# VectorE's convolution sums in PSUM, and a round plan for the work between scans

## The chip, the core and the metric

The kernel runs on one core of a Trainium2 chip. The core has TensorE (PE, matrix products, with its weight loads shown apart as PEld), VectorE (DVE), ScalarE (ACT), GpSimd (POOL) and the SyncE queue (SP), which here issues all DMAs. SBUF and PSUM are the on-chip memories; PE writes its results to PSUM. The metric is the device time of one execution in microseconds (us), the median of several runs; lower is better.

## What is computed

Four layers work on four images of 64x64 positions with 96 channels. The first two are state-space layers, the last two attention without softmax and a small feed-forward net with rounded values. The change concerns the first two (and, through a shared class, the start of the last two). One such layer, cut to what matters:

```python
xz = einsum('bhwc,ec->bhwe', group_norm(x), in_proj_w)      # 96 -> 2 x 192
xp, z = split(xz, 2)
xc = conv_general_dilated(xp, conv_w, 3x3, 'SAME', feature_group_count=192)
xc = silu(xc + conv_b)                                       # u in the kernel
xs = four orders of xc: by rows, by columns, and both reversed
delta, B, C = softplus(...), ..., ...                        # small products of xs
h_l = exp(delta_l * A) * h_(l-1) + delta_l * u_l * B_l       # 16 states per channel
y = sum over states of h * C, over the four orders, + D * u
y = layernorm(y) * w + b
y = y * silu(z)
x = x + einsum('bhwd,cd->bhwc', y, out_proj_w)
```

The convolution is depthwise: each channel is a sum of nine shifted copies of its image, each times a weight of that channel (nine "taps").

## The kernel before

**Units.** A layer takes the four images in two pairs, so there are four units (layer 0 pair 0, layer 0 pair 1, layer 1 pair 0, layer 1 pair 1). `PairScan` runs the recurrence of a unit over all positions, states and orders, in steps of 1024 positions. Before each scan stands a stage, `between_scans` (line 128). Before the first scan it only makes the inputs of unit 0. Before the other three it is "joint": `Inputs` makes the next unit's inputs while `Outputs` finishes the unit whose scan just ended. The outputs of the last unit are made in `token_layers`, by `one_by_one` (line 484), beside the start of the attention layers.

**Order.** `InOrder` (line 48) keeps each compute engine's instructions in the order in which the program issues them, so an instruction that waits holds up all behind it on its engine. SP's DMAs are not wrapped so; the framework places them.

**Inputs.** A pair's 192 channels of two images are held in three images `imgs[0..2]` of 128 partitions each (the third has the last 64 channels of both). The input comes in 16 pieces (`BEATS`) of 512 positions. `project` (line 302) multiplies a piece with the weights three times (PSUM tiles `ips`, tag `mm`), and ACT copies it out four times: twice into the images, twice through SiLU into `zs`, which goes to DRAM as `zg`. `fold` puts the group norm into the weights and `in_shift`, clears the images' borders and makes nine diagonal matrices `diag`.

**Convolution.** `jobs` (line 325) yields one tap at a time. `CONVS` names which rows of which image go to which engine, as (image, first row, rows):

- `vector`: nine DVE instructions over SBUF; the first multiplies and adds the bias, the others do `to = view * weight + to` (`SCALAR_TENSOR_TENSOR u<-img,par,u`). Sixteen rows make 128x1024 elements.
- `tensor`: nine products with `diag`, summed in a PSUM tile `cps`.
- `gpsimd`: ACT multiplies a tap into `parts`, POOL adds it to `u`.

After the taps ACT applies SiLU. `Handout` hands out taps by `SHARES`, a sixth of a beat's share at each of the six `fill()` calls of a beat.

**Outputs.** In groups `g` of 256 positions: load `zt`, `xr`, `ys`; `measure` (DVE statistics of `ys`), `scale` (through `rstd_of`, line 65: DVE adds epsilon into `ln_ve`, POOL takes the power -0.5 into `ln_rs`), `shift` (DVE), `normalise` (ACT, in place in `ys`), `turn` (PE transposes into `pt`), `scaled_back` (ACT, into `gt`), `gate` (POOL multiplies `gt` by `zt`), `project` (PE, into `po`), `store` (DVE adds `xr`, and takes the next norm's statistics `gn_stats`; in layer 1 ACT copies `po` instead). A beat of the loop in `between_scans` holds steps of the groups `beat - 1`, `beat` and `beat + 1`, with `fill()` between them. `close` ends the norm of the next layer's input.

**Start of the scan.** `scan.begin` makes the scan's first chunk of projections and its first `delta` and `du`; the loop takes a step of it at each `fill()` from beat `BEGIN` on. `other` collects, in the first stage only, the statistics of the second pair.

[...]A joint stage gives five to the tag `mm`, two to `pt`, one to `po`.

Of the kernel before, what the change touches and what calls it, by code (L numbers as in the profile page):

```python
# [9 lines left out]
F32 = mybir.dt.float32  # L10
# [54 lines left out]
def rstd_of(nc, pool, var, shape, tag, half):  # L65

    ve = pool.tile(shape, F32, name=f"{tag}_ve", bufs=4)
    nc.vector.tensor_scalar(ve, var, EPS, None, ALU.add)
    rs = pool.tile(shape, F32, name=f"{tag}_rs", bufs=4)
    nc.gpsimd.tensor_tensor(rs, ve, half, ALU.pow)  # L70
    return rs
# [55 lines left out]

def between_scans(tc, cst, ident, half, pn, u, before, scan, after):

    with ExitStack() as stage:  # L130
        nc = InOrder(tc)
        outs, other, joint = None, iter(()), before is not None
        pieces = PIECES[joint]
# [10 lines left out]
        ins.fold()  # L144
        convs = [Handout(ins.jobs(engine), share) for engine, share in SHARES[joint].items()]
        beginnings = scan.begin(nc, ins.pp)
        for beat in range(-LEAD, BEATS + 1):
            now = outs is not None and 0 <= beat < BEATS
            past = outs is not None and beat > 0
            ready = pieces[beat + LEAD]  # L150

            def fill():
                if beat >= BEGIN[joint]:
                    next(beginnings, None)
                if beat < BEATS:
                    for one in convs:
                        one.go(ready)

            if past:
                outs.gate(beat - 1)  # L160
            fill()
            if now:
                outs.normalise(beat)
            if outs is not None:
                for g in range(0 if beat == -LEAD else beat + 2, min(beat + 3, BEATS)):
                    outs.load(g)
                if 0 <= beat + 1 < BEATS:
                    outs.measure(beat + 1)
                    outs.scale(beat + 1)
            fill()  # L170
            for piece in range(*pieces[beat + LEAD : beat + LEAD + 2]):
                if piece + 4 < BEATS:
                    ins.load(piece + 4)
                ins.project(piece)
            fill()
            if now:
                outs.turn(beat)
                outs.scaled_back(beat)
            fill()
            if past:  # L180
                outs.project(beat - 1)
            ready = pieces[beat + LEAD + 1]
            fill()
            if past:
                outs.store(beat - 1)
            if outs is not None and 0 <= beat + 1 < BEATS:
                outs.shift(beat + 1)
            fill()
            if beat >= 3:
                next(other, None)  # L190
        for _ in beginnings:
            pass
        while any([one.go(BEATS) for one in convs]):
            pass
        if outs is not None:
            outs.close()
        for _ in other:
            pass
# [3 lines left out]
    False: (0, 3, 5, 7, 9, 11, 13, 15, 16, 16, 16, 16, 16, 16, 16, 16, 16, 16, 16, 16),  # L202
    True: (0, 3, 5, 6, 8, 9, 11, 12, 14, 15, 16, 16, 16, 16, 16, 16, 16, 16, 16, 16),
}
LEAD = 1
BEGIN = {False: 4, True: 8}

CONVS = {
    False: {'vector': ((0, 0, 16), (2, 0, 16), (0, 16, 16), (2, 16, 16), (0, 32, 16), (2, 32, 16), (2, 48, 16), (0, 48, 16), (1, 56, 8)), 'tensor': ((1, 0, 8), (1, 8, 8), (1, 16, 8), (1, 24, 8), (1, 32, 8), (1, 40, 8), (1, 48, 8))},
    True: {'vector': ((0, 0, 16), (2, 0, 16), (0, 16, 16), (2, 16, 16), (0, 32, 16), (2, 32, 16), (2, 48, 16), (0, 48, 8)), 'tensor': ((1, 0, 8), (1, 16, 8), (1, 32, 8), (1, 48, 8), (1, 40, 8)), 'gpsimd': ((1, 8, 8), (1, 24, 8), (1, 56, 8), (0, 56, 8))},  # L210
}
SHARES = {False: {'vector': 9, 'tensor': 6}, True: {'vector': 5, 'tensor': 3, 'gpsimd': 3}}

class Handout:
# [5 lines left out]
    def go(self, beat):  # L220
        self.owed = min(self.owed + self.share / 6, self.share)
        while self.owed >= 1 and self.ready is not None and beat >= self.ready:
            self.owed -= 1
            self.ready = next(self.pieces, None)
        return self.ready is not None

class Inputs:

    def __init__(self, nc, tc, stage, cst, ident, half, pn, u, spare, joint, layer, pr):
# [7 lines left out]
        self.pp = stage.enter_context(tc.tile_pool(name="a_ps", bufs=5, space=PSUM))  # L237
# [4 lines left out]
        self.xs, self.xns = {}, {}  # L242
# [59 lines left out]
    def project(self, beat):  # L302

        nc, (c, i) = self.nc, divmod(beat, 2)
        mine, other = slice(D1 * i, D1 * i + D1), slice(D1 - D1 * i, 128 - D1 * i)
        cols, rows = slice(512 * c, 512 * c + 512), slice(1 + 8 * c, 9 + 8 * c)
        xn, zg = self.xs.pop(beat), self.layer.zg[self.pr]
        pss = []
        for q in range(3):
            ps = self.pp.tile([128, 8, HW], F32, name=f"ips{q}", tag="mm")  # L310
            nc.tensor.matmul(ps, self.wi[:, i, 128 * q : 128 * q + 128], xn, start=True, stop=True)
            pss.append(ps)
        shift = self.shift[:, i]
# [10 lines left out]

    def jobs(self, engine):

        nc, par = self.nc, self.layer.par
        for j, row, n in CONVS[self.joint][engine]:
            s, cols = j // 2, slice(HW * row, HW * (row + n))
            last = min(HW // 8 - 1, (row + n) // 8)  # L330
            after = 2 * last + (j > 0) + 1
            to = self.u[j][:, cols].rearrange("p (h w) -> p h w", w=HW)
            bias = par[:, s, P_CB : P_CB + 1]
            yield after
            if engine == "tensor":
                to = self.pp.tile([128, 8, HW], F32, name="cps", tag="mm")
            for tap in range(9):
                dy, dx = divmod(tap, 3)
                v = self.imgs[j][:, row + dy : row + dy + n, dx : dx + HW]
                weight = par[:, s, P_CONV + tap : P_CONV + tap + 1]  # L340
                if engine == "tensor":
                    nc.tensor.matmul(to, self.diag[:, tap], v, start=(tap == 0), stop=(tap == 8))
                elif engine == "vector" and tap == 0:
                    nc.vector.tensor_scalar(to, v, weight, bias, ALU.mult, ALU.add)
                elif engine == "vector":
                    nc.vector.scalar_tensor_tensor(to, v, weight, to, ALU.mult, ALU.add)
                elif tap == 0:
                    nc.scalar.activation(to, v, AF.Identity, scale=weight, bias=bias)
                else:
                    part = self.parts[:, tap % 2]  # L350
                    nc.scalar.mul(part, v, weight)
                    nc.gpsimd.tensor_tensor(to, to, part, ALU.add)
                yield after
            if engine == "tensor":
                nc.scalar.activation(self.u[j][:, cols], to.rearrange("p h w -> p (h w)"), AF.Silu, bias=bias)
# [562 lines left out]
class Rounds:  # L918

    def __init__(self):  # L920
        self.tasks = {}
# [397 lines left out]
```

## Time and profile before

| | |
|---|---|
| median of 3 runs | 10450.39 us (10448.65 to 10457.71) |
| the profiled execution | 10456.78 us, of which its instructions span 10454.9 us |
| granted TensorE clock, mean | 0.887 of full speed |
| busy share of the span | PE 76%, PEld 56%, DVE 92%, ACT 84%, POOL 89% |
| scan, POOL `h<-h,cb` | 3072 instructions, 7194.7 us |
| scan, DVE `h<-da,last,bp` | 2064 instructions, 4736.2 us |
| first stage | to 160.65 us |
| joint stages | 2455.7 to 2657.0, 4955.7 to 5159.1, 7452.6 to 7640.8 us |
| chain that ended last, by engine | ACT 34%, issue 20%, DVE 17%, PE 16%, POOL 11% |

The stage boundaries are from the timeline: from the end of DVE's last scan instruction to the start of its first `bp` product for the next unit. Busy time counts an instruction from start to end, with any wait that it spends after it has started. A group of instructions is named by what it writes and reads (`u<-img,par,u`), with the shape of what it writes. Since the in-order wrapper issues every instruction, nearly all groups carry its line, L61, and are told apart by their tiles.

### The profile page before, as it was taken

The numbers are of one execution on the slowest core, as the hardware profiler recorded it, in microseconds if no ns is written. First come the engines' busy times: TensorE is split into PE (matmuls) and PEld (weight loads), VectorE is DVE, ScalarE is ACT, GpSimd is POOL, SyncE is SP. The second block draws the span as 40 slices with busy tenths as digits, with TensorE's granted clock in tenths as the row PEclk, the third lists the DMA queues.
The fourth block names the chain that finished last, engine by engine and source line by source line (L and its number), as shares of the span: only waits on it lengthen the run. The fifth ranks groups of instructions, "written<-read, shape, count | busy, mean of one in ns | idle before, by whom it ended". The sixth has DMA issues, their size and how long they took to land.

```text
span 10454.9 us, 142148 instructions
## 1 busy us (share of the span) xinstructions
PE 7920.4 (76%) x47500; PEld 5900.9 (56%) x47500; DVE 9648.0 (92%) x6803; ACT 8817.8 (84%) x18798; POOL 9255.7 (89%) x5402
## 2 busy tenths in 40 slices
PE   7777777777777777777777777777777777777767
PEld 4655555554555555555455555555556555555555
DVE  8999999999999999999899999999899999999957
ACT  6888888887888888888788888888888888888868
POOL 3999999997899999999699999999789999999946
PEclk9898998988888998888888989898988898988978
DMA  4677777776577777777477777777757777777730
GB/s 138 205 213 215 218 221 219 221 220 185 185 211 210 219 221 213 219 219 215 160 207 212 218 214 218 223 218 220 203 178 209 215 217 218 218 218 220 219 104 25
DMA packets 903380, 2117.24 MB, mean 203 GB/s; under 512 B 330326, under 2 KB 639896, under 8 KB 704920
## 3 DMA queue, kind: packets, MB, share of 16 engines
q1 hardware_dynamic: 902648, 2108.15, 68.8%
q8 instruction: 377, 6.18, 0.3%
q14 instruction: 355, 2.91, 0.1%
HBM read 1946.42 MB, written 161.48 MB: 202 GB/s over the span
## 4 chain that ended last, share of the span: by engine, by line
ACT 34%; issue 20%; DVE 17%; PE 16%; POOL 11%; DMA 2%; SPq 1%; DVEq 0%; POOLq 0%; ACTq 0%
ACT x L61 14%; ACT da L61 12%; DVE h L61 9%; POOL h L61 8%; PE yp L61 6%; PE bp L61 5%; DVE bp L61 4%; ACT bp L61 2%; DVE u L61 1%; PE xps L61 1%; POOL dbu L61 1%; DMA cb<-crow 1%; PE dps L61 1%; ACT L61 1%; PE dups L61 1%
## 5 line engine op out<-in xcount | busy, mean ns | idle before, releaser
L61 POOL TENSOR_TENSOR h<-h,cb 128x1024 f32<-128x1024 f32 x3072 | 7194.7, 2366 | 230.5 <-issue 64.0
L61 DVE TENSOR_TENSOR_SCAN h<-da,last,bp 128x1024 f32<-128x1024 f32 x2064 | 4736.2, 2335 | 143.8 <-PE bp L61 19.7
L61 ACT ACTIVATE x<-dut,bt 128x128 f32<-128x128 f32 x12288 | 3495.0, 370 | 1.5 <-PE bp L61 1.3
L61 PE MATMUL yp<-ident,h 128*128 128x128 f32 x24576 | 3351.3, 296 | 10.5 <-POOL h L61 10.5
L61 PEld LDWEIGHTS yp<-ident,h 128*128 128x128 f32 x24576 | 3177.9, 156 | 125.7 <-issue 74.3
L61 ACT ACTIVATE da<-delta,amat 128x1024 f32<-128x1024 f32 x2752 | 3060.4, 1138 | 103.0 <-DVE h L61 97.8
L61 PE MATMUL bp<-ident,x 128*128 128x128 f32 x10240 | 1670.4, 315 | 1293.0 <-DVE h L61 950.2
L61 PEld LDWEIGHTS bp<-ident,x 128*128 128x128 f32 x10240 | 1352.8, 162 | 1857.3 <-ACT x L61 1004.3
L61 DVE TENSOR_TENSOR bp<-du,bp 128x1024 f32<-128x1024 f32 x1472 | 1780.1, 1213 | 260.8 <-PE bp L61 259.2
L61 DVE TENSOR_TENSOR_SCAN h<-da,bp 128x1024 f32<-128x1024 f32 x688 | 1537.5, 2274 | 45.6 <-ACT da L61 4.6
L61 PE MATMUL bp<-bparts,sel 96*128 96x512 bf16 x2944 | 924.7, 400 | 761.4 <-DVE h L61 742.7
L61 PEld LDWEIGHTS <-sel 96*128 96x128 bf16 x2944 | 226.3, 100 | 1557.9 <-DVE h L61 1048.7
L61 ACT ACTIVATE bp<-delta,amat 128x1024 f32<-128x1024 f32 x320 | 358.1, 1119 | 528.0 <-DVE h L61 526.2
L61 POOL TENSOR_TENSOR dbu<-du,bb 128x1024 f32<-128x1024 f32 x320 | 754.9, 2359 | 0.0
L61 DVE TENSOR_TENSOR_SCAN h<-bp,last,dbu 128x1024 f32<-128x1024 f32 x240 | 558.9, 2329 | 13.4 <-POOL dbu L61 12.7
L61 PE MATMUL xps<-u,wx 128*76 128x512 f32 x768 | 556.8, 811 | 0.0
L61 ACT ACT_TABLE_LOAD x392 | 502.9, 1283 | 11.3 <-DMA x<-xo 4.4
L61 POOL COPY last<-h 128x2 f32<-128x2 f32 x1152 | 215.4, 187 | 326.7 <-DVE h L61 309.8
L61 POOL TENSOR_TENSOR du<-delta,u 128x1024 f32<-128x1024 f32 x188 | 496.6, 2642 | 0.0
L61 PE MATMUL dps<-cdt,wdt 12*128 12x512 f32 x768 | 442.4, 656 | 0.0
L61 ACT COPY ysum<-yp 128x1024 f32<-128x1024 f32 x192 | 194.4, 1012 | 284.7 <-PE yp L61 284.7
L61 ACT COPY dut<-dups 128x512 f32<-128x512 f32 x384 | 220.6, 574 | 239.7 <-PE dups L61 239.7
(141 smaller groups left out, 6296.9 us busy)
## 6 DMA issues: line engine op xcount, KB each, us to landing
cb<-crow SPq DMA_DIRECT2D x1024, 1024.0 KB
cb<-crow SPq DMA_DIRECT2D x1024, 512.0 KB
bb<-crow SPq DMA_DIRECT2D x384, 256.0 KB
bb<-crow SPq DMA_DIRECT2D x128, 512.0 KB
y<-ysum SPq DMA_DIRECT2D x192, 256.0 KB
kept<-y SPq DMA_DIRECT2D x160, 256.0 KB
y<-ysum SPq DMA_DIRECT2D x64, 512.0 KB
zt<-zg SPq DMA_DIRECT2D x64, 384.0 KB
```

Of the source, the lines that this page charges most:

```text
L61: return self.tc.keep_in_program_order(getattr(self.engine, op)(*args, **kwargs))
```

## The change

Three things change together.

**The vector chunks.** They are all eight rows high (128x512 elements). ACT makes the first tap with the bias, into a PSUM tile `vps`[...]; DVE adds the other eight taps there; ACT's SiLU reads PSUM and writes `u`. The next chunk's first tap is issued after the fifth tap of the present one, and a chunk's SiLU after the fourth tap of the next. In a joint stage one chunk, (0, 56, 8), moves from `gpsimd` to `vector`.

**The order.** The six-part beats are replaced by a list of rounds (`Rounds`, moved up in the file). `plan` gives each step of an output group a round of its own, two rounds from group to group, with the load six rounds ahead of `measure`. A piece's products (`multiply`) and ACT's copies of it (`spread`) stand a round apart, and its taps may begin a round later. Every round ends with the handout of taps and, from round `BEGIN` on, one step of the scan's beginning. GpSimd's addition is handed out one step after ACT's product. The tail's `one_by_one` uses the same `plan`, which loads groups two rounds earlier than before.

**Small moves.** `ln_ve` goes to the engine that gates, POOL in joint stages and DVE in the tail. `po` shares the two buffers of `pt`; `mm` has four buffers in a joint stage and six in the first.

```diff
-def rstd_of(nc, pool, var, shape, tag, half):
+def rstd_of(nc, pool, var, shape, tag, half, engine):
-    nc.vector.tensor_scalar(ve, var, EPS, None, ALU.add)
+    engine.tensor_scalar(ve, var, EPS, None, ALU.add)
...
         ins.fold()
+        rounds, ready = Rounds(), {}
+        if outs is not None:
+            outs.plan(rounds, OUTS_FROM)
+        for piece in range(BEATS):
+            r = PIECES[joint][piece]
+            if piece + 4 < BEATS:
+                rounds.at(r, ins.load, piece + 4)
+            rounds.at(r, ins.multiply, piece)
+            rounds.at(r + 1, ins.spread, piece)
+            ready[r + 2] = piece + 1
         convs = [Handout(ins.jobs(engine), share) for engine, share in SHARES[joint].items()]
-        beginnings = scan.begin(nc, ins.pp)
-        for beat in range(-LEAD, BEATS + 1):
...
+        beginnings, pieces = scan.begin(nc, ins.pp), 0
+        for r, _ in enumerate(rounds.run()):
+            pieces = ready.get(r, pieces)
+            for one in convs:
+                one.go(pieces)
+            if r >= BEGIN[joint]:
+                next(beginnings, None)
+            if r >= 3:
                 next(other, None)
+        while any([one.go(BEATS) for one in convs]):
+            next(beginnings, None)
...
 PIECES = {
+    False: (0, 1, 3, 4, 6, 7, 9, 10, 12, 13, 15, 16, 18, 19, 21, 22),
+    True: (0, 2, 4, 6, 8, 10, 12, 14, 16, 18, 20, 22, 24, 26, 28, 30),
 }
+OUTS_FROM = 6
+PER_GROUP = 2
+BEGIN = {False: 10, True: 18}
...
-SHARES = {False: {'vector': 9, 'tensor': 6}, True: {'vector': 5, 'tensor': 3, 'gpsimd': 3}}
+SHARES = {False: {'vector': 6, 'tensor': 2.5}, True: {'vector': 4, 'tensor': 1.4, 'gpsimd': 1}}
...
-        self.pp = stage.enter_context(tc.tile_pool(name="a_ps", bufs=5, space=PSUM))
+        self.pp = stage.enter_context(tc.tile_pool(name="a_ps", bufs=4 if joint else 6, space=PSUM))
...
                 else:
                     part = self.parts[:, tap % 2]
                     nc.scalar.mul(part, v, weight)
-                    nc.gpsimd.tensor_tensor(to, to, part, ALU.add)
+                    yield after
+                    nc.gpsimd.tensor_tensor(rows, rows, part, ALU.add)
+                    continue
                 yield after
...
+    def vector_jobs(self, chunks):
+
+        nc, sums = self.nc, {}
+
+        def begin(i):
+            _, _, views, weights, bias = chunks[i]
+            sums[i] = self.pp.tile([128, 8, HW], F32, name="vps", bufs=2)
+            nc.scalar.activation(sums[i], views[0], AF.Identity, scale=weights[0], bias=bias)
+
+        def end(i):
+            nc.scalar.activation(chunks[i][1], sums.pop(i).rearrange("p h w -> p (h w)"), AF.Silu)
+
+        yield chunks[0][0]
+        begin(0)
+        for i, (after, _, views, weights, _) in enumerate(chunks):
+            for tap in range(1, 9):
+                yield after
+                nc.vector.scalar_tensor_tensor(sums[i], views[tap], weights[tap], sums[i], ALU.mult, ALU.add)
+                if tap == 4 and i > 0:
+                    end(i - 1)
+                if tap == 5 and i + 1 < len(chunks):
+                    yield chunks[i + 1][0]
+                    begin(i + 1)
+        yield BEATS
+        end(len(chunks) - 1)
...
+    def plan(self, rounds, start):
+        for g in range(BEATS):
+            rounds.at(max(start + PER_GROUP * g - 6, 0), self.load, g)
+            for r, task in enumerate((
+                self.measure, self.scale, self.shift, self.normalise, self.turn, self.scaled_back, self.gate,
+                self.project, self.store,
+            )):
+                rounds.at(start + PER_GROUP * g + r, task, g)
...
     def one_by_one(self):
         rounds = Rounds()
...
+        self.plan(rounds, 4)
         yield from rounds.run()
```

In `CONVS` a joint stage has 16 vector chunks of eight rows (before: seven of sixteen and one of eight), five tensor chunks (unchanged) and three for GpSimd (before: four). The first stage has 17 vector chunks of eight rows (before: eight of sixteen and one of eight) and seven tensor chunks (unchanged).

## The prediction

> **What bounds the kernel.** I read the busy digits of the page first, then busy time by stretch around the dips, then the groups of those stretches, and last their timeline.
>
> ```profile
> DVE  8999999999999999999899999999899999999957
> POOL 3999999997899999999699999999789999999946
> ```
>
> POOL has a dip at the start and three more, a quarter of the span apart. These are the stretches between scans, the only places that the change touches before the tail; the scans keep their instructions. From the timeline (last scan instruction on DVE to the first `bp` product of the next unit) they last to 160.65 us at the start, then 2455.7 to 2657.0 (201 us), 4955.7 to 5159.1 (203) and 7452.6 to 7640.8 (188): 753 us, 7% of the span, are in play. Columns: busy us and count per engine, granted clock, DMA share, GB/s.
>
> ```profile
> core 0: us, PE busy (x) PEld busy (x) DVE busy (x) ACT busy (x) POOL busy (x), PEclk, DMA share, GB/s
> 27.00:160.00 133.00, 113.88 (x271) 48.79 (x271) 106.86 (x108) 64.67 (x94) 0.52 (x1) 0.95 0.21 67
> 2459.00:2657.00 198.00, 154.75 (x474) 80.80 (x472) 168.80 (x291) 138.49 (x238) 115.65 (x77) 0.87 0.49 144
> 4959.00:5159.00 200.00, 158.68 (x475) 84.32 (x473) 167.55 (x291) 138.25 (x238) 115.15 (x77) 0.85 0.49 143
> 7456.00:7641.00 185.00, 156.93 (x662) 92.84 (x659) 154.32 (x237) 142.68 (x252) 114.71 (x76) 0.89 0.53 155
> ```
>
> In each joint stretch DVE leads, but PE is 14 and 9 us behind in the first two and 3 ahead in the last, and ACT is at 70 to 77%. DVE can fall only until these two stop it. Next, DVE's groups (count, then busy us, mean ns, then idle before): the first stretch has no POOL work, the second has.
>
> ```profile
> L61 DVE SCALAR_TENSOR_TENSOR u<-img,par,u 128x1024 f32<-128x1024 f32 x64 | 82.1, 1283 | 2.5
> ...
> L61 DVE SCALAR_TENSOR_TENSOR u<-img,par,u 128x1024 f32<-128x1024 f32 x56 | 90.7, 1619 | 1.3
> ...
> L61 DVE TENSOR_SCALAR ln_ve<-ymv 128x4 f32<-128x4 f32 x16 | 11.3, 705 | 0.5
> L61 DVE TENSOR_TENSOR xo<-xr,po 96x512 f32<-96x512 f32 x16 | 10.8, 677 | 11.0 <-PE po L61 11.0
> L61 DVE SCALAR_TENSOR_TENSOR u<-img,par,u 128x512 f32<-128x512 f32 x8 | 8.5, 1064 | 0.2
> ...
> L61 DVE TENSOR_TENSOR du<-delta,u 128x1024 f32<-128x1024 f32 x1 | 1.2, 1219 | 0.0
> ```
>
> The same tap costs 1283 ns alone and 1619 ns beside POOL: 56 x 0.336 = 19 us of a joint stretch is waiting inside instructions. `ln_ve`, four elements wide, needs 705 ns there. Over the whole page a product with one operand in SBUF and one in PSUM shows nothing of it, though POOL is 89% busy:
>
> ```profile
> L61 DVE TENSOR_TENSOR bp<-du,bp 128x1024 f32<-128x1024 f32 x1472 | 1780.1, 1213 | 260.8 <-PE bp L61 259.2
> ```
>
> **The taps.** In place of 7 chunks of 16 rows and one of 8 (`vector` in a joint stretch), there are 16 of 8 rows (one taken over from GpSimd), with eight DVE taps each. Half-width taps without interference follow each other thus:
>
> ```profile
> 2463.65 0.17 DVE L61 TENSOR_SCALAR in_shift<-shps 128x6 f32<-128x6 f32 x1 [4.95 <-ACT diag L61]
> ...
> 2474.01 0.81 DVE L61 TENSOR_SCALAR u<-img,par 128x1024 f32<-128x1024 f32 x1
> ...
> 2643.90 3.11 DVE L61 SCALAR_TENSOR_TENSOR u<-img,par,u 128x512 f32<-128x512 f32 x4
> ...
> 2657.01 1.23 DVE L61 TENSOR_TENSOR bp<-du,bp 128x1024 f32<-128x1024 f32 x1 [1.19 <-PE bp L61]
> ```
>
> Four take 3.11 us, 0.78 each. No tap with its sum in PSUM stands in the trace; nearest is `bp<-du,bp`, 1213 ns against 1219 for `du<-delta,u` in SBUF: the same. [...]I take the row, which has the same engine, type and placement[...]. So a joint stretch pays 128 x 0.78 = 100 us; before it was 90.7 + 8.5 + 8.7 (first taps) = 108 and some 2 us between them: **10 us off DVE**. The wait saved (19) is mostly spent on the smaller width (112 x 0.78 = 87 against 56 x 1.32 = 74).
>
> In the first stretch nothing interfered: 82.1 + 6.0 + 7.0 + 2.5 between = 98 becomes 136 x 0.78 = 106, **8 us more**.
>
> **Other moves off DVE and on to ACT.** `ln_ve` goes to POOL: 11 us off DVE. POOL's price for it lies between 0.19 us (its `last` copy, 128x2) and 0.49 (its 128x96 tensor-scalar): 3 to 8 us, under cover of its 82 us idle in that stretch, and it gives up 8 additions of 1.6 us. DVE then has 168.8 - 10 - 11 = 147 us of work. ACT gets the first taps and smaller activations:
>
> ```profile
> L61 ACT ACTIVATE u<-cps,par 128x512 f32<-128x512 f32 x5 | 3.4, 681 | 6.2 <-PE cps L61 6.2
> L61 ACT ACTIVATE u<-img,par 128x512 f32<-128x512 f32 x4 | 3.2, 809 | 0.0
> ```
>
> 16 first taps x 0.81 + 16 SiLU from PSUM x 0.68 = 24 us, less the old SiLUs (7.4 + 0.6) and one GpSimd chunk (8 x 0.716 + 0.81 + 0.63 = 7.2): 138.5 + 9 = 147 us. PE keeps its work, 155 us as modelled[...]. Three engines now stand near 150: the stretch is decided by how they wait for each other.
>
> **The order, in rounds.** I lay the new plan out in pairs of rounds (one output group, one input piece). DVE in a full pair: 8 taps 6.2, four `ystats` 1.13, `ymv` 0.36, `shift` 0.14, `xo` 0.67, `gn_stats` 0.75: 9.3 us. ACT: normalise 1.85, scale back 1.23, a piece's four copies 2.65, first tap and SiLU 1.3, GpSimd's products 1.3, rest 0.8: 9.1. With both so full I allow 9.8 (estimate). The present loop takes (2651 - 2474)/16 = 11.1 per group. Full pairs are rounds 12 to 31, 10 x 9.8 = 98; rounds 6 to 11, where ACT's pieces limit, 14; 32 to 36 (no more pieces) 2.5 x 9.5 = 24; 37 to 44 (mostly taps) 28: 164 us. DVE's first tap comes after three pieces and ACT's first tap, 11.6 us after `in_shift` (now 10.4): 2475.2. With the closing norm, about 4 us as now, `bp` comes at 2643 in place of 2657: **-14**. The third stretch, from its own `in_shift` at 4964.26: 5144 for 5159, **-15**. In the fourth DVE has no `xo` and `gn_stats`, ACT copies `xo` (0.47 a group) and sets the pair, again 9.8 or 9.9: 14 + 99 + 21 + 27 = 161, from 7472.2, and 1.2 for `bp`: 7634 for 7641, **-6**.
>
> First stretch: DVE starts at 42 for 37.85, since ACT's first tap stands behind four pieces; 106 of taps, 8 of image 1's statistics left over, 3.5 of small work, 3 of waits give 162.5 for 160.65: **+2**. The statistics and norm that now follow the last tap (154.3 to 160.6) move into the loop, or it would be +8.
>
> **Queues and buffers moved past.** The skew's rounds are hidden where another group's work fills them. SP's transfers are not held to program order, only the engines' instructions; each output load still waits for a buffer three groups back, so asking six rounds ahead costs and gains nothing inside a stretch, and the 6.7 us that DVE waits for `ys` now moves under the six rounds of start-up. In PSUM, `pt` and `po` share two buffers, and a joint stretch has four `mm` for five. A transposition then waits for `xo` of the same round on DVE; behind it on PE stand the piece's products, and ACT waits for those. I charge that in the 9.8. The tail's loads come two rounds earlier: 0, with 15 us (DVE's longest wait for `ys` there, 9961 to 9977) as the best case and 5 us as the worst.
>
> Sum: +2 - 14 - 15 - 6 = **-33 us**, on the profiled execution's 10456.8 (span 10454.9 and 1.9 around it): 10424. The runs' median, 10450.4, lies 6.4 under that execution; the same -33 there gives **10417**.
>
> **Rivals.** First, the skew frees the engines nearly down to their work: 147 us from 2468 plus start and close, some -28 in each of the two middle stretches, -20 in the last, 0 at the start, -14 in the tail: 10360. For it: `xo` waited 11 us for `po`, POOL 24 for `ln_ve`, ACT 18 for DVE's sums, and all of these are put behind their producers. Against: PE needs 155, in a clock of 0.87. Second, **no change**: [...]ACT at its limit (a pair at 10.9, 10 x 1.1 x 3 = 33) takes the gain: 10450. Third, **slower**: PE runs out of PSUM. A piece's products need three of four `mm` buffers while a convolution sum holds one and, from round 19, a projection holds another; the third product then waits until ACT has got past its scaling (1.23) to the piece's first copy (0.68), and the product itself (0.43) comes late: 2.34 us. Paid in each of ten full pairs of three stretches it is 70 us: 10487. It decides from 1.1 us per pair on (33 / 30). For it: PE already waits 10 us for ACT's `img` with five buffers. Against: before round 19 four are enough, and PE has a third of each pair free.
>
> **Chances.** Forecast 0.50 (10390 to 10435 by itself), freed engines 0.22, no change 0.16, slower 0.12. A measurement tells about 0.2%, 21 us, from no change; with the upper edge of the forecast's range lying inside that: faster 0.70, same 0.18, slower 0.12. Range 10350 to 10452: it leaves out the slower case and little of the first rival's lower end.
>
> **What would show it.** Half-width taps at 0.74 to 0.76 us whatever POOL does (0.81 or more: the rule was right); DVE at 147 and ACT at 147 us per joint stretch; no `ln_ve` on DVE; first `bp` at about 162, and stretches of 187, 188 and 182 us. PE idle before `ips` behind ACT's `img` would show the third rival. The forecast is wrong if the pair isn't set by DVE and ACT, or if the tail moves by over 10 us.

## The result, and the profile after

| | before | after |
|---|---|---|
| median of 6 runs each | 10456.43 us (10448.65 to 10462.45) | 10395.94 us (10385.07 to 10401.45) |
| ratio, 95% interval | | 0.9941 (0.9928 to 0.9954) |
| span of the profiled execution | 10454.9 us | 10395.6 us |
| first stage | 160.6 us | 166.8 us |
| joint stages | 201.3, 203.3, 188.2 us | 183.8, 186.5, 169.6 us |
| four scans, sum | 9180.7 us | 9178.9 us |
| from the last scan to the end (tail) | 520.8 us | 510.1 us |

Stages are counted as in the prediction, from the end of DVE's last scan instruction to its first `bp`. The time fell by 60 us where 33 were forecast. In the spans: +6.2 in the first stage, -17.5, -16.8 and -18.6 in the joint ones, -1.8 in the scans and -10.7 in the tail.

The busy digits of the page, in 40 slices, of the changed kernel: POOL's dips are still there, since the joint stages are still there, but 17 to 19 us shorter.

```profile
DVE  8999999998999999999899999999899999999957
POOL 3999999996899999999599999999789999999946
```

Busy time in the four stretches of the changed kernel (columns as before: the window and its length, busy us and count of PE, PEld, DVE, ACT, POOL, granted clock, DMA share, GB/s):

```profile
27.00:166.00 139.00, 116.92 (x275) 51.50 (x275) 113.38 (x163) 77.89 (x118) 0.70 (x1) 0.91 0.21 66
2464.00:2645.00 181.00, 151.04 (x476) 77.74 (x475) 142.89 (x332) 143.08 (x252) 80.94 (x85) 0.91 0.53 158
4939.00:5122.00 183.00, 151.11 (x474) 77.58 (x472) 143.42 (x331) 142.67 (x252) 80.92 (x85) 0.91 0.53 156
7421.00:7587.00 166.00, 145.26 (x661) 86.62 (x659) 126.72 (x276) 148.15 (x267) 80.59 (x84) 0.97 0.60 173
```

In the second row DVE has 143 us for 169 before, ACT 143 for 138, PE 151 for 155, POOL 81 for 116. DVE no longer leads. The three engines that the forecast saw near 150 stand at 143 to 151, 79 to 83% of the stretch each, and PE in front. In the last row ACT leads, at 89%.

The groups of that second stretch, of DVE, ACT and POOL (count, then busy us, mean ns, then idle before and what ended it):

```profile
L61 DVE SCALAR_TENSOR_TENSOR vps<-img,par,vps 128x512 f32<-128x512 f32 x128 | 95.1, 751 | 9.9 <-ACT vps L61 6.5
...
L61 DVE TENSOR_TENSOR xo<-xr,po 96x512 f32<-96x512 f32 x16 | 10.8, 678 | 12.6 <-PE po L61 12.6
...
L61 ACT ACTIVATE ys<-ys,shift,ln_rs 128x192 f32<-128x192 f32 x64 | 29.7, 543 | 0.0
...
L61 ACT ACTIVATE vps<-img,par 128x512 f32<-128x512 f32 x16 | 12.5, 780 | 0.2
...
L61 ACT ACTIVATE u<-vps 128x512 f32<-128x512 f32 x16 | 9.4, 588 | 14.9 <-DVE vps L61 14.9
...
L61 POOL TENSOR_TENSOR u<-u,parts 128x512 f32<-128x512 f32 x24 | 30.5, 1271 | 26.3 <-ACT parts L61 26.3
L61 POOL TENSOR_TENSOR gt<-gt,zt 128x768 f32<-128x768 f32 x16 | 29.2, 1828 | 2.9 <-ACT gt L61 2.8
L61 POOL TENSOR_TENSOR ln_rs<-ln_ve,half 128x4 f32<-128x4 f32 x16 | 16.6, 1037 | 1.3
L61 POOL TENSOR_SCALAR ln_ve<-ymv 128x4 f32<-128x4 f32 x16 | 3.7, 228 | 54.4 <-DVE ymv L61 54.4
```

The tap costs 751 ns beside a POOL that is busy for 45% of the stretch. POOL's own instructions are shorter as well; these are the rows of the kernel before, in this stage:

```profile
L61 POOL TENSOR_TENSOR u<-u,parts 128x512 f32<-128x512 f32 x32 | 52.2, 1631 | 36.5 <-ACT parts L61 29.8 <-DMA ys<-y 6.2
L61 POOL TENSOR_TENSOR gt<-gt,zt 128x768 f32<-128x768 f32 x16 | 32.9, 2057 | 14.1 <-ACT gt L61 8.4 <-issue 5.7
L61 POOL TENSOR_TENSOR ln_rs<-ln_ve,half 128x4 f32<-128x4 f32 x16 | 29.8, 1861 | 24.1 <-DVE ln_ve L61 23.9
```

The addition went from 1631 ns to 1271, the gate from 2057 to 1828, the power from 1861 to 1037. The `ys` row of the changed kernel ends with 0.0: ACT's normalisation never waits, where it waited 11.4 us for `shift` before. POOL's 54 us before `ln_ve` are idle time of an engine that has half of the stage to spare.

The first stage is longer. Its timeline on DVE in the changed kernel (start, us, instruction, and in brackets the idle time before it):

```profile
28.76 0.17 DVE L61 TENSOR_SCALAR in_shift<-shps 128x6 f32<-128x6 f32 x1 [2.48 <-PE shps L61]
28.84 2.46 DVE L61 BATCH_NORM_STATS2 gn_stats<-xt 96x6 f32<-96x512 f32 x4
44.56 1.62 DVE L61 SCALAR_TENSOR_TENSOR vps<-img,par,vps 128x512 f32<-128x512 f32 x2 [13.26 <-ACT vps L61]
...
166.80 1.23 DVE L61 TENSOR_TENSOR bp<-du,bp 128x1024 f32<-128x1024 f32 x1 [3.82 <-PE bp L61]
```

DVE's first tap stands at 44.56 (it stood at 37.85): DVE waits 13.3 us for ACT, which makes four pieces' copies before it makes the first tap. At the end DVE waits 3.8 us for `bp`, where it waited 1.3.

### The profile page after: what moved, and what is told of

Read it like the earlier page. It is cut to its first block, busy times and chain, and to the rows that moved or that the text cites. A ratio compares the mean times of both kernels' runs of the same rounds, so it can differ in the third digit from the quotient of the medians.

```text
span 10395.6 us, 142356 instructions
## 1 busy us (share of the span) xinstructions
PE 7902.8 (76%) x47500; PEld 5890.1 (57%) x47500; DVE 9576.3 (92%) x6978; ACT 8844.7 (85%) x18865; POOL 9153.7 (88%) x5426
## 4 chain that ended last, share of the span: by engine, by line
ACT 39%; issue 18%; PE 17%; DVE 17%; POOL 7%; DMA 2%; SPq 0%; DVEq 0%; POOLq 0%; ACTq 0%
ACT x L61 16%; ACT da L61 14%; DVE h L61 10%; PE yp L61 6%; PE bp L61 5%; POOL h L61 5%; DVE bp L61 4%; ACT bp L61 2%; PE xps L61 2%; DVE vps L61 1%; ACT L61 1%; PE dps L61 1%; PE dups L61 1%; POOL dbu L61 1%; ACT dut L61 1%
## 5 line engine op out<-in xcount | busy, mean ns | idle before, releaser
L61 PE MATMUL yp<-ident,h 128*128 128x128 f32 x24576 | 3353.8, 296 | 10.2 <-POOL h L61 10.2
L61 DVE TENSOR_TENSOR_SCAN h<-bp,last,dbu 128x1024 f32<-128x1024 f32 x240 | 558.8, 2328 | 11.4 <-POOL dbu L61 10.7
L61 ACT ACT_TABLE_LOAD x392 | 502.9, 1283 | 6.9
L61 DVE SCALAR_TENSOR_TENSOR vps<-img,par,vps 128x512 f32<-128x512 f32 x520 | 387.1, 752 | 51.1 <-ACT vps L61 36.6
```

What stands on the lines that cost most here:

```text
L61: return self.tc.keep_in_program_order(getattr(self.engine, op)(*args, **kwargs))
```

## The experiments

Two explanations stood against each other for the joint stages. By the first, the gain comes from where the sums are: with its sum in PSUM a tap no longer waits while POOL works. By the second, it comes from the order: a consumer that stands a round behind its producer doesn't stop its engine. Separate questions were the tail, the first stage and `ln_ve`. Stage times below are from one profiled execution of each kernel. Each comparison had its own runs of the kernel before, so ratios are to those.

### 1. The new order, the sums in SBUF

```diff
-            sums[i] = self.pp.tile([128, 8, HW], F32, name="vps", bufs=2)
+            sums[i] = chunks[i][1].rearrange("p (h w) -> p h w", w=HW)
...
-            nc.scalar.activation(chunks[i][1], sums.pop(i).rearrange("p h w -> p (h w)"), AF.Silu)
+            nc.scalar.activation(chunks[i][1], chunks[i][1], AF.Silu)
```

> The changed kernel with one thing undone: the vector chunks' sums lie in SBUF (in u, eight rows, first tap by ACT) and not in PSUM; order, buffers and ln_ve stay. Theory A (PSUM keeps DVE's taps clear of POOL, and the order alone would bring little): beside POOL a tap costs about 1.06 us as the half-width taps before the change did, in place of 0.75, so each joint stage has 128 x 0.31 = 40 us more of DVE and POOL slows too; joint stages 205 to 225 us for 184, 186 and 170, time about 10480 to 10510. Theory B (the order did it): joint stages within 4 us of the changed kernel's, time 10390 to 10410. The first stage has no POOL work and stays at 167 us within 2 by both.

Measured: 10484.06 us, ratio 1.0022 (1.0015 to 1.0028). First stage 165.4, joint stages 212.9, 214.6 and 195.6, tail 509.8. The second stretch of this kernel, its window row, and then, from its groups, a DVE and two POOL rows:

```profile
2464.00:2680.00 216.00, 164.86 (x483) 84.80 (x483) 191.63 (x335) 151.13 (x267) 104.42 (x87) 0.83 0.48 144
```

```profile
L61 DVE SCALAR_TENSOR_TENSOR u<-img,par,u 128x512 f32<-128x512 f32 x128 | 138.6, 1089 | 10.2 <-ACT u L61 6.7
...
L61 POOL TENSOR_TENSOR u<-u,parts 128x512 f32<-128x512 f32 x24 | 36.3, 1514 | 13.2 <-ACT parts L61 13.2
L61 POOL TENSOR_TENSOR gt<-gt,zt 128x768 f32<-128x768 f32 x16 | 34.1, 2130 | 2.1 <-ACT gt L61 2.1
```

The same 128 taps in the same order take 138.6 us for 95.1. That is 43 us of DVE a stage, and DVE is at 89% of its window (85% in the kernel before). The two rows of POOL grow too, by 17 to 19%. In the first stage, where POOL stands still, the edit gains and costs next to nothing (165.4 for 166.8). So the place of the sum is worth 26 to 29 us of each joint stage, at this width and in this order, and it is worth that only where POOL works. (Chunks of sixteen rows lose less to SBUF: 1562 ns a tap in experiment 4 for 1283 beside an idle POOL, where those of eight rows take 1089 for 752.) How the two engines come to stretch each other isn't shown; that they do is, by 1089 ns a tap against 751.

### 2 and 3. The sums in PSUM, the old order

The kernel before, with the new chunks and `vector_jobs`, in the old six-part beats; `ln_ve` stays on DVE, the tail loads as before. To make room for the sums, `po` shares the two buffers of `pt` and `mm` has four in a joint stage, as in the changed kernel.

```diff
-SHARES = {False: {'vector': 9, 'tensor': 6}, True: {'vector': 5, 'tensor': 3, 'gpsimd': 3}}
+SHARES = {False: {'vector': 18, 'tensor': 6}, True: {'vector': 10, 'tensor': 3, 'gpsimd': 3}}
...
-        self.pp = stage.enter_context(tc.tile_pool(name="a_ps", bufs=5, space=PSUM))
+        self.pp = stage.enter_context(tc.tile_pool(name="a_ps", bufs=4 if joint else 6, space=PSUM))
...
+        if engine == "vector":
+            yield from self.vector_jobs()
+            return
...
-            self.sums[g] = po = self.pp.tile([C, 2, 256], F32, name="po", tag=self.summed, bufs=bufs)
+            self.sums[g] = po = self.pp.tile([C, 2, 256], F32, name="po", tag=self.summed)
```

> The kernel before with one part of the change alone: vector sums in PSUM, first tap by ACT, in the old six-part beats (mm four buffers, po sharing pt, ln_ve on DVE). Theory A (PSUM taps carry the joint stages' gain): taps at 0.75 us, DVE 10 to 15 us lower, joint stages about 190, 192 and 178, time near 10425. Theory B (the order carries it): joint stages at 201, 203 and 188 or longer, since the old order leaves ACT's first taps and PE's fewer buffers in the way; time 10455 to 10500. The tail stays at 521 us by both.

Measured: 10495.52 us, ratio 1.003 (1.0019 to 1.0042), slower than before. First stage 174.7 (14 us more), joint stages 208.1, 207.6 and 196.9 (20 us more together). The taps are as fast as in the changed kernel (753 ns), and DVE has 153.9 us of work in a window of 206. Here is what the engines wait for in the second stage (us in total, times, longest):

```profile
ACT ys L61 <- DVE shift L61: 28.4, 14, 4.5
DVE xo L61 <- PE po L61: 24.4, 10, 5.2
...
PE po L61 <- ACT gt L61: 21.3, 13, 3.9
```

ACT's normalisation waits for DVE's `shift` in 14 groups of 16, PE's projection for ACT's `gt` in 13, DVE's `xo` for the projection in 10. In the changed kernel these three are none, 4.2 us and 12.6 us; in the kernel before, with DVE busy for 169 of 198 us, they were 11.4 us (6 times), none and 11.0. The fewer PSUM buffers don't explain the loss: PE waits 6.3 us for ACT's copies to `img`, which free `mm` (10.2 before), and the profile shows no wait of PE for `xo`, which frees the shared pair. The end of the stage on DVE's timeline:

```profile
2650.95 3.92 DVE L61 SCALAR_TENSOR_TENSOR vps<-img,par,vps 128x512 f32<-128x512 f32 x5
...
2668.25 0.68 DVE L61 TENSOR_TENSOR xo<-xr,po 96x512 f32<-96x512 f32 x1 [5.21 <-PE po L61]
```

The last tap ends at 2654.9, and `bp` comes 21.6 us later. The taps were used up, and the last groups run their chain with nothing beside it. That is partly a matter of the share, so the next run hands out fewer taps a beat:

```diff
-SHARES = {False: {'vector': 18, 'tensor': 6}, True: {'vector': 10, 'tensor': 3, 'gpsimd': 3}}
+SHARES = {False: {'vector': 15, 'tensor': 6}, True: {'vector': 9, 'tensor': 3, 'gpsimd': 3}}
```

> As the run with PSUM sums in the old order, but 9 vector taps a beat in place of 10 (15 for 18 in the first stage), so that the taps last as long as the output groups. If that run's 207 us came from taps that ended 22 us before the stage (no work left to hide the output chain): joint stages 195 to 201, time 10440 to 10470. If the old order's chain (each step right behind its producer) sets the pace whatever DVE does: still 203 to 208, time 10480 to 10500.

Measured: 10474.07 us, ratio 1.0012 (1.0006 to 1.0019); first stage 164.1, joint stages 204.2, 202.4 and 195.0. The bare end shrinks to 13.0 us in the second stage (10.0 in the kernel before), but the last tap ends 191.1 us into the stage, where it ended after 191.3 us before. (In the other two joint stages it ends after 188.8 for 192.3 and 185.9 for 180.9.) DVE had some 15 us less to do (153.9 in the window of the run before this one, 168.8 in the kernel before), and the loop ran no faster. The three waits are still there, 30.5, 17.9 and 21.4 us. In the old order DVE's spare time becomes waiting in the chain from engine to engine. Of the two expectations the second is the nearer by the stages; the time lies between the two. Only two shares were tried.

### 4. The new order, the old chunks

The changed kernel with chunks of sixteen rows, all taps on DVE in SBUF, and the old chunk lists. `ln_ve` stays on POOL and the tail keeps its early loads, so these two are part of what is called the order alone here.

```diff
-SHARES = {False: {'vector': 6, 'tensor': 2.5}, True: {'vector': 4, 'tensor': 1.4, 'gpsimd': 1}}
+SHARES = {False: {'vector': 3.2, 'tensor': 2.5}, True: {'vector': 2.6, 'tensor': 1.4, 'gpsimd': 1.4}}
...
-        self.pp = stage.enter_context(tc.tile_pool(name="a_ps", bufs=4 if joint else 6, space=PSUM))
+        self.pp = stage.enter_context(tc.tile_pool(name="a_ps", bufs=5 if joint else 8, space=PSUM))
...
+                elif engine == "vector" and tap == 0:
+                    nc.vector.tensor_scalar(rows, v, weight, bias, ALU.mult, ALU.add)
+                elif engine == "vector":
+                    nc.vector.scalar_tensor_tensor(rows, v, weight, rows, ALU.mult, ALU.add)
```

> The changed kernel's rounds and buffers for the work between scans, but the vector chunks of before in every stage: sixteen rows, nine taps on DVE, sums in SBUF, one chunk of eight rows back at GpSimd (2.6 taps a round for vector, 1.4 for gpsimd; mm with five buffers). So the order, ln_ve on POOL and the tail's loads alone. Theory A (DVE's load of some 158 to 168 us still bounds a joint stage, so the order alone gains only what DVE idled, about 10 us of 29): joint stages 188 to 198, time 10415 to 10440. Theory B (order is the whole of the gain): joint stages at 184 to 187 and 170, time near 10390. Theory C (waiting on POOL grows when the work is packed tighter): joint stages over 200, time over 10440.

Measured: 10421.48 us, ratio 0.9964 (0.995 to 0.9978). First stage 152.5, joint stages 194.9, 191.0 and 186.7, tail 509.4. The window of the second stage, and two rows of its groups on DVE:

```profile
2452.00:2650.00 198.00, 156.66 (x484) 82.16 (x484) 164.37 (x279) 139.09 (x238) 132.80 (x95) 0.87 0.50 146
```

```profile
L61 DVE SCALAR_TENSOR_TENSOR u<-img,par,u 128x1024 f32<-128x1024 f32 x56 | 87.5, 1562 | 1.8
...
L61 DVE SCALAR_TENSOR_TENSOR shift<-ymv,ln_rs 128x4 f32<-128x4 f32 x16 | 9.3, 580 | 3.0 <-POOL ln_rs L61 3.0
```

The order alone is a gain, but of 20 us in the joint stages (6.4, 12.3, 1.5), with DVE at 83% and full of waiting inside its instructions: 1562 ns for a tap that takes 1283 beside an idle POOL, and 580 for a `shift` that takes 144 in the changed kernel. In the middle of the stage DVE has nothing left to give:

```profile
2500.00:2600.00 100.00, 80.17 (x260) 42.80 (x261) 95.84 (x163) 71.53 (x126) 77.15 (x46) 0.90 0.57 174
```

Only one set of shares was tried in this run, and its first tap came 20 us after `in_shift` (10.4 in the kernel before, 12.7 in the changed one), 9 to 11 us later than before in each of the three stages, so the order may be worth more than 20.

Joint stages together, against before (sum of three): the order alone -20, the sums in PSUM alone +9 (with the better share), both -53. So up to some 42 us (53 - 20 + 9) belong to neither part by itself; less, if the late first taps of this run cost it time. Beside the wide chunks of this run the sums in PSUM are worth 33 us over the three stages (572.6 to 539.8), beside the narrow ones of experiment 1 they were 83. **The place of the sums frees DVE; the order is what can use a free DVE.**

### 5. `ln_ve` back on DVE

```diff
-        rs = rstd_of(nc, self.p2, mv[:, :, :, 1], [128, 2, 2], "ln", half, self.gating)
+        rs = rstd_of(nc, self.p2, mv[:, :, :, 1], [128, 2, 2], "ln", half, nc.vector)
```

> The changed kernel with ln_ve back on DVE in the joint stages. As the prediction priced it, 705 ns each beside POOL: 11 us of DVE per joint stage, so stages 4 to 11 us longer and time 10405 to 10425. If its price was a wait for POOL that the PSUM taps removed: 0.18 us each, 3 us of DVE per stage, and the stages within 4 us of the changed kernel's, time 10390 to 10405.

Measured: 10399.65 us, ratio 0.9941 (0.9927 to 0.9956), the changed kernel's ratio. Joint stages 182.0, 182.1 and 168.6. A row of DVE's groups in the second stage:

```profile
L61 DVE TENSOR_SCALAR ln_ve<-ymv 128x4 f32<-128x4 f32 x16 | 2.7, 166 | 0.0
```

The instruction that took 705 ns on DVE takes 166 there. The mean of 705 hid two kinds. In the kernel before, eight of the sixteen took 0.17 us. The other eight met a POOL instruction that was running, and each of them ended 0.03 us after that one had; six took 1.4 to 1.6 us. Here is one, with the gate that it met:

```profile
2517.56 1.80 POOL L61 TENSOR_TENSOR gt<-gt,zt 128x768 f32<-128x768 f32 x1
2517.83 1.55 DVE L61 TENSOR_SCALAR ln_ve<-ymv 128x4 f32<-128x4 f32 x1
```

In this run none of the sixteen meets a gate (in the fourth stage five meet POOL, and the mean there is 294 ns). So it isn't the instruction that was dear, nor directly the place of the taps' sums, but what ran on POOL at that moment. Why the gates no longer fall there wasn't traced. Moving `ln_ve` to POOL shows no gain here beside the rest of the change; experiment 8 comes back to it.

### 6. The tail with the old loads

```diff
-    def plan(self, rounds, start):
+    def plan(self, rounds, start, ahead=6):
         for g in range(BEATS):
-            rounds.at(max(start + PER_GROUP * g - 6, 0), self.load, g)
+            rounds.at(max(start + PER_GROUP * g - ahead, 0), self.load, g)
...
-        self.plan(rounds, 4)
+        self.plan(rounds, 4, 4)
```

> The changed kernel with the tail's output groups loaded at their old place (four rounds ahead of measure in place of six); nothing else differs. If the tail's 10.6 us (521 to 510) come from the earlier loads: tail back at 519 to 522 us, time about 10406. If they come from elsewhere (where the scan happens to end): tail 508 to 512, time as the changed kernel's.

Measured: 10407.27 us, ratio 0.9947 (0.9932 to 0.9962); tail 517.0 for 510.1 (519 or more if the loads were the whole of it), the rest within 3 us a stage of the changed kernel. The last gate of the outputs ends 120.0 us after the last scan (before 121.0, changed kernel 111.7). So some 7 or 8 of the tail's 10.7 us are the earlier loads. What they change is seen on DVE's timeline; first the kernel before, then the changed one:

```profile
9976.65 0.36 DVE L61 BATCH_NORM_STATS2 ystats<-ys 128x6 f32<-128x192 f32 x1 [15.13 <-DMA ys<-y]
```

```profile
9932.78 0.36 DVE L61 BATCH_NORM_STATS2 ystats<-ys 128x6 f32<-128x192 f32 x1 [16.48 <-DMA ys<-y]
```

The wait is as long as before, but falls on the fifth group instead of the fourth: SP issues the attention layers' weights nearly in one go (9953.9 to 9969.0 us in the kernel before, 9909.4 to 9925.4 in the changed one), and now one group's load more stands ahead of them (four groups' `ys`, where three stood). All waits for `ys` in the tail together are 27.5 us for 32.9. Why the rest of the tail moved isn't settled: tails of kernels with the same plan lie between 509.4 and 514.0 us.

### 7. The first stage as it was, and the tail's weights later

The changed kernel with the first stage's sums in SBUF in the old chunks, pieces a little earlier, eight `mm` buffers there.

```diff
-    False: (0, 1, 3, 4, 6, 7, 9, 10, 12, 13, 15, 16, 18, 19, 21, 22),
+    False: (0, 1, 2, 3, 4, 6, 7, 9, 10, 12, 13, 15, 16, 18, 19, 21),
...
-SHARES = {False: {'vector': 6, 'tensor': 2.5}, True: {'vector': 4, 'tensor': 1.4, 'gpsimd': 1}}
+SHARES = {False: {'vector': 3.2, 'tensor': 2.5}, True: {'vector': 4, 'tensor': 1.4, 'gpsimd': 1}}
...
-        if engine == "vector":
+        if engine == "vector" and self.joint:
```

> The changed kernel with the first stage's vector chunks as before the change (sixteen rows, all nine taps on DVE, sums in SBUF, 3.2 taps a round), mm with eight buffers there, pieces slightly earlier. If the first stage lost its 6 us to DVE's narrower taps and to the later first tap: it falls from 167 to 152 to 160 us, time about 10385. If PE and the scan's beginning set its end: it stays within 3 us of 167 and the time within 3 of the changed kernel's.

Measured: 10386.29 us, ratio 0.9926 (0.9909 to 0.9942). First stage 155.0 us, the joint ones 183.3, 183.4 and 172.9. DVE's timeline in that stage:

```profile
40.38 0.81 DVE L61 TENSOR_SCALAR u<-img,par 128x1024 f32<-128x1024 f32 x1 [5.33 <-ACT img L61]
...
155.03 1.22 DVE L61 TENSOR_TENSOR bp<-du,bp 128x1024 f32<-128x1024 f32 x1
```

DVE starts 4 us earlier, its taps (all nine of a chunk) take 95.0 us for 101.3 (eight of nine), and it no longer waits before `bp`. One more edit on top of this one issues the tail's layer weights eight rounds of the outputs later:

```diff
         load(1)
+        for _ in range(8):
+            next(outs)
         wa = [weights(attention_weights, n, ("wq", "wkv", "Wff", "bff")) for n in (2, 3)]
```

> A version meant to beat both: the run with the first stage's chunks in SBUF, and in the tail the weights of the attention and feed-forward layers issued on SP after eight more rounds of the outputs, since 16 us of SP's weight transfers stand before the loads of output group 4 and DVE waits 16.5 us for it there. If that wait is on the path: tail 497 to 505 us, time about 10373. If the image that follows waits for the weights, or the DMA only moves the wait: tail within 4 us of 512, time 10382 to 10390.

Measured: 10399.26 us, ratio 0.9942 (0.9927 to 0.9957). The tail grows to 527.0 us, longer than either expectation had it (497 to 505, or about 512). DVE still waits 33.1 us for `ys`, and ACT's first `tn` of the attention work starts 74.9 us into the tail for 58.6. The wait in the tail isn't saved in this way.

### 8. Together, on one chip

The changed kernel, the one with the old first stage, and that one with `ln_ve` on DVE, once more, five runs each.

> The changed kernel as it is, beside the next two on the same chip. If its gain is what the first comparison gave, the ratio to the kernel before lies at 0.993 to 0.995 (about 10395 us).

> The changed kernel with the first stage's sums back in SBUF in sixteen rows, once more. If PSUM sums and ACT's first tap only cost time where GpSimd stands still, it is again 8 to 12 us below the changed kernel of this same comparison (ratio about 0.001 lower). If the earlier 10 us were a spread between comparisons, the two agree within 4 us.

> The same, with ln_ve back on VectorE too. If moving ln_ve brings nothing once the taps are in PSUM (166 ns each on VectorE), it is within 5 us of the kernel of the run before it; if GpSimd's wait for ymv (54 us a stage) was hidden but ln_ve on VectorE delays the chain in the tail or the last stage, it is some 5 to 10 us slower.

| | median (lowest to highest) | ratio to before | first stage | joint stages | scans | tail |
|---|---|---|---|---|---|---|
| changed kernel | 10391.6 (10382.35 to 10397.01) | 0.9943 (0.9929 to 0.9957) | 166.2 | 183.1, 183.7, 173.2 | 9164.4 | 509.9 |
| old first stage | 10378.88 (10374.51 to 10381.63) | 0.993 (0.9917 to 0.9942) | 152.1 | 183.7, 183.8, 173.9 | 9165.5 | 513.7 |
| and `ln_ve` on DVE | 10391.76 (10375.96 to 10393.14) | 0.9939 (0.9927 to 0.9952) | 153.3 | 185.4, 185.1, 173.6 | 9183.5 | 510.3 |

The old first stage is the fastest version measured: all its five runs lie below all five of the changed kernel, its median by 12.7 us, where 8 to 12 were expected. The two profiled executions differ by 7.9 us: 14.1 less in the first stage, 3.8 more in the tail and 2.4 more between; why the tail is longer isn't shown. The intervals of the two ratios overlap. `ln_ve` on DVE missed both its expectations by the median (12.9 us more, where under 5 or 5 to 10 stood). In the profile its joint stages differ by 3 us in all, and 18 us stand in the scans, which the edit leaves alone. Scans of one and the same kernel differed nearly as much, if between two chips: 9178.9 and 9164.4 us in the two profiles of the changed kernel. Whether `ln_ve` costs a few us is left open.

## Why the prediction was right, and where it was short

The direction and what bounds the joint stages were right; the size was 27 us short. Some 18 of these lie in the joint stages and 11 in the tail, the scans moved by 2, and the first stage went 4 the other way.

**What bounds the joint stages** was right. DVE led because its taps waited inside themselves; with this gone three engines stand nearly level: DVE 143 and ACT 143 us, where 147 each were forecast, and PE 151.

**The price of PSUM** was right as the row had it. In the first stage, POOL idle, a half-width tap takes 755 ns with its sum in PSUM (changed kernel) and 752 in SBUF (experiment 7):

```profile
L61 DVE SCALAR_TENSOR_TENSOR vps<-img,par,vps 128x512 f32<-128x512 f32 x136 | 101.3, 755 | 19.5 <-ACT vps L61 15.3
...
L61 DVE SCALAR_TENSOR_TENSOR u<-img,par,u 128x512 f32<-128x512 f32 x8 | 6.0, 752 | 0.3
```

So a tap of this width shows no price of PSUM beyond these 3 ns.

**`ln_ve`** was wrong in its kind: 11 us were to come off DVE by the move. Nearly 9 of them go without it (11.3 to 2.7 us, experiment 5), in the old order too (180 ns each in the second stage of experiment 2). The forecast took 705 ns for the price of the instruction; with 0.17 us each for the instances that met nothing, 8.6 of the row's 11.3 us were waiting for POOL, nearly all for its gate. That DVE's sum held all the same is luck: both edits were made at once, and either takes most of that time off DVE.

**The order** was right in kind, and more is due to it than the prediction says, which gave the gain to DVE's work and used the rounds only to lay it out. Without the order the saved work gives a loss of 9 to 20 us in the joint stages (experiments 2 and 3).

**The pair of rounds** is the term that was mis-sized. "With both so full I allow 9.8": from the first to the eleventh gate on POOL (rounds 12 to 32) the ten pairs take 94.9, 96.0 and 91.2 us, so 9.5, 9.6 and 9.1; in experiment 8's profile of the same kernel 94.1, 94.7 and 91.6. The engines' busy time in these three windows:

```profile
2493.90:2588.80 94.90, 83.55 (x264) 42.19 (x263) 78.67 (x190) 82.11 (x149) 50.41 (x46) 0.93 0.63 191
4969.90:5065.90 96.00, 83.89 (x268) 42.95 (x267) 78.00 (x188) 82.11 (x149) 50.41 (x47) 0.95 0.64 192
7446.50:7537.70 91.20, 79.79 (x366) 47.26 (x365) 71.55 (x164) 84.02 (x154) 50.43 (x47) 0.98 0.65 194
```

Neither was as full as laid out. Of a pair DVE has 7.9 us in the second stage (9.3), ACT 8.2 (9.1), and PE has 8.4. Two of the causes can be counted. "8 taps 6.2" took every step of the handout for a tap, but a chunk takes nine steps, eight taps and the start of the next chunk on ACT: the ten pairs hold 70, 68 and 71 taps, not 80. And "GpSimd's products 1.3" are 16 in ten pairs, 1.1 us each pair. ACT's two new terms were too dear besides: the first tap 0.780 us for 0.81, the SiLU 0.588 for 0.68. So the pair isn't set by DVE and ACT, as the forecast said that it must be. In the second and third stages PE, ACT and DVE are busy for 81 to 88% of it, PE most; in the fourth ACT leads at 92%. How much of the 9.8 each cause took away isn't separated.

The rest of the second stage came as laid out: the first tap 12.7 us after `in_shift` (11.6), 12.3 to round 12 (14), 52.0 from round 32 to the last tap (52), 4.0 to close (4). The fourth stage was furthest off, -18.6 for -6. Eight of the 12 missing us are the pair (91.2 for 99), 3 the rounds before it (10.9 for 14), 2 its later rounds (46.1 for 48) and 1 an earlier `in_shift`, less 2 for a later close (3.4 for 1.2). The granted clock was higher there too (0.97 over the stage for 0.89 before), and what that gave isn't separated. The changed kernel's second profile, at 173.2 us, gave this stage 15 us less than before and not 18.6; its pairs were as short, but `in_shift` came 1.2 us later and the first tap 1.4 us later behind it.

**The first stage** cost 6.2 for 2. DVE's first tap came 2.6 us later than laid out (44.6 for 42), and its waits after that were 6.2 us among the taps and 3.8 before `bp` where 3 were allowed in all; the taps themselves took 101.3 us for the 106 priced.

**The tail** was put at 0, from -15 to +5; it was -10.7. That is 11 of the 60 us from a term put at nothing, and by the forecast's own sign ("if the tail moves by over 10 us") it missed here. "Asking six rounds ahead costs and gains nothing" was said of a stretch; in the tail the loads share SP with the layers' weights, and one group got ahead of them (experiment 6). The rest of the tail's gain is open.

**The rivals.** PE running out of PSUM wasn't seen: in the second stage PE waited 5.0 us for ACT's `img` with four buffers, 10.2 before with five. The pair that `pt` and `po` share cost it 6.2 us of waiting for `xo`. The measured -60 lies half way between the forecast (-33) and the freed engines (-90): the joint stages gave 53 us, where the one had 35 and the other 76, and the tail 11, where they had 0 and 14.

## What to carry to other kernels

Before a step is moved off an engine because it is slow there, ask whether it is slow by itself: look at its single instances and at what ran on the neighbour, since a mean can hide a fast half and a waiting half (`ln_ve`, 705 ns: eight of sixteen at 0.17 us, eight that met POOL). Where two engines stretched each other's instructions with both at work in SBUF (a tap 1089 ns, GpSimd's addition 1514), moving one operand to PSUM freed both (751 and 1271); where the neighbour was idle it gained nothing (755 ns for 752), and the narrower chunks cost time (taps of 101.3 us for 95.0). Work saved on the leading engine counts only as far as the order lets the others follow (experiments 2 and 3: some 15 us less on DVE in the second stage, and the three joint stages 9 to 20 us longer together): look at the waits of consumers right behind their producers, and put a round between them first. And when a plan is priced by its steps, count in the changed kernel's own lists which steps are work of which engine.

## What the runs showed of the hardware that wasn't expected

- The stretch is mutual. With both tensors of a tap in SBUF, DVE's taps go from 751 to 1089 ns and POOL's additions from 1271 to 1514, its power of four elements from 1037 to 1443 (new order, second stage). With the sum in PSUM the tap costs what it costs beside an idle POOL (755).
- Small instructions of DVE paid for the moment, not for the place of the taps' sums. `shift`, four elements with two SBUF inputs, took 0.14 to 0.18 us when it met nothing; in the kernel before and the changed one, every `shift` over 0.2 us in a joint stage ended 0.02 us after the end of the POOL instruction that was running when it started. Its mean in the second stage was 580 ns in experiment 4 and 176 in experiment 1, both with the sums in SBUF, and 411 in experiment 2 and 144 in the changed kernel, both with the sums in PSUM. In the changed kernel's fourth stage seven of sixteen met POOL (mean 436).
- `ln_ve` reads one tensor and waited for POOL's gate in the same way (1.4 to 1.6 us in six of sixteen, experiment 5).
- ACT's SiLU of 128x512 from PSUM took 588 ns without a bias operand and 674 with one, in the second stage of the changed kernel.
